# Cross-attention with Winograd products on one core: the last batch's closing order, and one reciprocal's place in the second batch

## The chip, the core and the metric

The kernel runs on one core of a Trainium2 chip. A core has five engines with instruction queues of their own: TensorE (PE; its weight loads are listed as PEld), VectorE (DVE), ScalarE (ACT), GpSimd (POOL) and SyncE (SP). Each works through its queue in order and waits on semaphores for the others. TensorE writes to eight PSUM banks, each of 128 partitions by 512 fp32 values; VectorE and ScalarE read and write the banks, and DMAs move data between the on-chip memory and HBM. The metric is the time on the device, in microseconds (us); the kernel before takes 672.67 us (median of three runs, 672.03 to 672.9).

## The reference

Eight batches of cross-attention, all in fp32. x1 is `x` and x2 is `ctx_2048`, both of shape (8, 512, 1024).

```python
q = jnp.einsum('bcn,dc->bnd', x1, Wq) + bq            # d = 64
k = jnp.einsum('bcn,dc->bdn', x2, Wk) + bk[:, None]
v = jnp.einsum('bcn,dc->bdn', x2, Wv) + bv[:, None]
attn = jax.nn.softmax(jnp.einsum('bnd,bdm->bnm', q, k), axis=2)
out = jnp.einsum('bcm,bnm->bcn', v, attn) + x1
```

For each of the 1024 columns n of x1, the scores against the 1024 columns m of x2 go through a softmax over m; the result is the weighted sum of the values, plus x1.

## The kernel before, in words

Batches are worked one after the other (`period(s, n, nn, nnn)`: s is the batch at hand, n, nn and nnn are the next ones), and every period also holds the scores, exponentials and first sums of batch n. The order of the instructions on each engine is written out by hand: instructions stand in each queue in the order in which the code calls them. Tiles are named by a tag, and a tile that takes a tag again waits until the tile before it has been read.

Two matrix products carry the work. First Y = x2 times the exponentials of the scores (`multiply`, `multiply_seeded` with stage "y"), then out = Wv times Y, scaled by the softmax's sums (stage "o"). Both are computed in 2 x 2 blocks by seven products in place of eight (Strassen's scheme in Winograd's form), in the order 1, 2, 6, 7, 5, 3, 4; some products are split in the same way once more (`inner_product`). Blocks are accumulated in PSUM: the pairs of banks "a0", "a1" and "c0", "c1" (the tags of `ps_a`), and two buffers "sc" (`ps_s`). Each bank of a pair holds one row tile j = 0, 1 of 128 rows by 512 columns. In the last batch `o_bank` swaps a and c in the second stage.

The last batch's second stage, as far as the change reaches: product 1 is put into bank pair c, product 6 is added to it and copied out by ScalarE (`s.tmp[6]`, tile `uo`), product 5 is added and copied out (`s.tmp[5]`, tile `uo`, L600), product 3 completes block 12 there. Product 7 is computed in pair a by `multiply_57` from inner products, interleaved with 5 and 3; VectorE completes its second row (L623). Block 22 is pair a plus `tmp[5]`; then product 4 is added to pair a, and block 21 is pair a plus `tmp[6]`. `evict_o` adds the bias and x1 (tile `s.x`, called `x_in_x_dram` in the trace), writes into that tile, and stores it with DMAs of 256 KB from SyncE. For blocks 22 and 21 it evicts both rows with bias and x1 (L739), then adds the parts and stores each row (L743, L744). TensorE's order there is product 3's first row, product 4 (both rows, L469), then product 3's second row in two halves (`rest`, L591), and block 12 is evicted last (L731), its second row in two halves, one stored by ScalarE and one by SyncE (L734).

In the second batch (`s.b == 1`) the sums of the softmax's denominators are reduced over partitions on GpSimd (L297), a small DMA takes 512 of them into a tile `few` of 128 x 4 (L299), VectorE inverts it (`invert`, L305, RECIPROCAL), GpSimd stores it as a row (L307), and `spread` reads it back to all partitions (L312). `shares` is both calls. Behind `shares(s, 1)` stand on VectorE the sums for the inner products of product 3: `right_stream` (L532, L537, L539, block sums of 128x1024 and 128x512) and `left_stream` (L517), which `weave` interleaves; then `lower` (L327), the completion of product 7 (`complete_7`, L661) and, on ScalarE, the negated copies of product 7 (`copy_7`, L671) and the copies between the inner steps of product 3 (L646).

Of the kernel before, what the change touches and what calls it, by code (L numbers as in the profile page):

```python
# [15 lines left out]
def kernel(  # L16
# [47 lines left out]
    nc = tc.nc  # L64
# [387 lines left out]
    def multiply(s, stage, i, left, right, n_k, last=False, hook=None, rows=range(2)):  # L452

        ka, kb, bank, opens = MULT[i]
        if stage == "o":
            bank = o_bank(s, bank)
            if i == 2:
                bank, opens = "p", False  # L460
        for j in rows:
            if opens:
                s.bank[bank, j] = ps_a.tile(
                    [P, H], F32, tag=f"{bank}{j}", name=f"ps_{stage}{bank}{j}_{s.b}_{i}"
                )
            ps = s.bank[bank, j]
            for n in HALVES if last and j else (slice(0, H),):
                for k in range(n_k):
                    nc.tensor.matmul(  # L469
                        ps[:, n],  # L470
                        left[ka][:, k, ts(j, P)],
                        right[kb][:, k, n],
                        start=opens and k == 0,
                        stop=i in (2, 3, 4) and k == n_k - 1,
                        skip_group_check=True,
                    )
# [100 lines left out]
    def multiply_57(s):  # L577

        s.inner["o7"] = inner_w["o7"]
        on, fresh = o_bank(s, "a"), o_bank(s, "c")  # L580
        bank = [ps_a.tile([P, H], F32, tag=f"{fresh}{j}", name=f"ps_o{fresh}{j}_{s.b}_7") for j in range(2)]
        s.bank[fresh, 0], s.bank[fresh, 1] = b0, b1 = bank
        chain, third = inner_parts(s, "o7")
        v = sb.tile([P, 2, H], F32, tag="aI3", name=f"vo7_{s.b}")[:, 0, left]
        s.tmp[5] = sb.tile([P, 2, H], F32, tag="u5", name=f"uo5_{s.b}")

        def plain(i, j, *ks, parts=(slice(0, H),)):
            ps, (ka, kb) = s.bank[on, j], (("S1", "T1"), ("S4", "22"))[i == 3]
            for n in parts:
                for k in ks:  # L590
                    nc.tensor.matmul(  # L591
                        ps[:, n],
                        w[ka][:, k, ts(j, P)],
                        s.y[kb][:, k, n],
                        start=False,
                        stop=i == 3 and k == 1,
                        skip_group_check=True,
                    )
            if i == 5 and 1 in ks:
                nc.scalar.copy(s.tmp[5][:, j, :], ps)  # L600
# [10 lines left out]
        nc.scalar.copy(b1[:, right], chain)  # L611
        plain(3, 0, 0)
        inner_product(s, "o7", 3, b0[:, right], False)
        plain(3, 0, 1)
        if s.b < B - 1:
            plain(3, 1, 0, 1)

        def rest():
            plain(3, 1, 0, 1, parts=HALVES)

        def complete():
            b = b1.rearrange("p (a n) -> p a n", a=2)
            nc.vector.tensor_tensor(b, b, v.unsqueeze(1).to_broadcast([P, 2, H // 2]), ALU.add)  # L623

        return complete, rest

    def multiply_seeded(s, i, v_tag, hooks={}, bank=None):

# [75 lines left out]
    def add_x1(s, k):  # L704

        nc.gpsimd.dma_start(s.tmp[RESULT[k][1]], block(s, k, x1), accum_op=ALU.add)

    def evict_o(s, k, hook=None):


# [4 lines left out]
        def bias(j):  # L715
            return bv_sb[:, 2 * r + j : 2 * r + j + 1]

        if s.b == B - 1 and k == "11":
            o = s.x[:, 0:2, ts(h, H)]
            for j in range(2):  # L720
                nc.vector.scalar_tensor_tensor(
                    o[:, j, :], s.bank[bank, j], bias(j), o[:, j, :], ALU.add, ALU.add
                )
                nc.sync.dma_start(out[s.b, ts(j, P), ts(h, H)], o[:, j, :])
            return
        if s.b == B - 1 and add is None:
            for j, n, engine in (
                (0, slice(0, H), nc.sync), (1, left, nc.scalar), (1, right, nc.sync)
            ):
                o = s.x[:, 2 * r + j, ts(h, H)][:, n]  # L730
                nc.vector.scalar_tensor_tensor(  # L731
                    o, s.bank[bank, j][:, n], bias(j), o, ALU.add, ALU.add
                )
                engine.dma_start(out[s.b, ts(2 * r + j, P), ts(h, H)][:, n], o)  # L734
            return
        if s.b == B - 1:
            o = s.x[:, 2 * r : 2 * r + 2, ts(h, H)]
            for j in range(2):
                nc.vector.scalar_tensor_tensor(  # L739
                    o[:, j, :], s.bank[bank, j], bias(j), o[:, j, :], ALU.add, ALU.add  # L740
                )
            for j in range(2):
                nc.vector.tensor_tensor(o[:, j, :], o[:, j, :], s.tmp[add][:, j, :], ALU.add)  # L743
# [20 lines left out]
        if hook is None and k in ("12", "22"):  # L764
            return leave
        leave()

    def add_tile(s, h, i):
        nc.gpsimd.dma_start(s.mx[h], s.e[h][:, :, i, :], accum_op=ALU.add)  # L769
# [148 lines left out]
    def period(s, n, nn, nnn):  # L918
# [7 lines left out]
        def second(i):  # L926
            if i == 1:
                multiply_o1(s)
            else:
                multiply(s, "o", i, w, s.y, 2, n is None and i == 3)  # L930

        def next_queries():
            evict = queries(nn, "c0")
# [98 lines left out]
        else:  # L1032
# [63 lines left out]
                s, 5, "r" if s.six else "top", {6: evict_q} if five else {}, "a"  # L1096
            )
            complete_5()
            shares(s, 1)
            if n is None:  # L1100
                for leave in s.leave:
                    leave()
            if n:
                weave(right_stream(s, 3, s.t["22"], "eT1"), left_stream(s, 3, s.a["S4"], "aI3"))
                lower(n, 0, 0)
            else:
                inner_right(s, 3, s.t["22"], "eT1")
# [140 lines left out]
                lower(n, 1, 3)  # L1248
                sum_y(s, "T4")
        if late:  # L1250
            complete_7, rest = multiply_57(s)
            if five:
                exponential(n, 1, 2)
                exponential(n, 1, 3)
# [84 lines left out]
```

## Time and profile before

| | |
|---|---|
| median of three runs | 672.67 us (672.03 to 672.9) |
| the profiled execution | 672.91 us |
| its span | 671.1 us |
| TensorE busy | 662.9 us, 99% |
| VectorE busy | 606.6 us, 90% |
| ScalarE busy | 363.2 us, 54% |
| GpSimd busy | 225.1 us, 34% |

The profiled execution's time is 1.8 us over its span. The span is the time from the first to the last event that the profiler recorded, and all positions below count from its start. A row of the timeline has the start, the time, the engine, the line of the kernel, the operation with what it writes and reads, its shape, how many instructions were merged, and in brackets the engine's idle time before it and what ended it. An fp32 matmul call shows as two matmul rows (two of 0.43 us for 512 columns). Rows with SPq or ACTq are DMA issues.

### The profile page before, as it was taken

To read this page: it belongs to the slowest core of one execution; us is meant where nothing else is said; L and a number is where in the kernel's file an instruction comes from. 1 tells how busy PE (TensorE), PEld (TensorE's weight loads), DVE (VectorE), ACT (ScalarE), POOL (GpSimd) and SP (SyncE) were. 2 spreads that over 40 slices of the span, in tenths; PEclk is the share of its full clock that TensorE was granted. 3 is DMA by queue.
4 is the path that set the end of the run, shared out by engine and by line. 5 is a ranking of instruction groups with operands and counts; after the bars stand their busy time and mean duration, and the time that the engine had idled before them with its cause. 6 is when DMAs were issued, how large, how long until landed. Compare 5 with 4: busy or idle time off the path is not lost.

```text
span 671.1 us, 7760 instructions
## 1 busy us (share of the span) xinstructions
PE 662.9 (99%) x2582; PEld 423.6 (63%) x2582; DVE 606.6 (90%) x828; ACT 363.2 (54%) x636; POOL 225.1 (34%) x196
## 2 busy tenths in 40 slices
PE   9999999999999999999999999999999999999996
PEld 5435754756558665677657685576855767566853
DVE  1989999899999899989999989998998988989974
ACT  2755466446565575464755647645576346554320
POOL 0125215630355312553134421454133450245300
PEclk9999999999999999999999999999999999999999
DMA  9679577995999859998699895999969990688522
GB/s 310 269 209 310 137 244 130 200 240 179 243 211 210 232 162 302 186 242 212 157 280 205 212 255 156 248 217 203 269 116 231 172 308 23 125 156 189 100 89 95
DMA packets 51960, 134.81 MB, mean 201 GB/s; under 512 B 5712, under 2 KB 8272, under 8 KB 51920
## 3 DMA queue, kind: packets, MB, share of 16 engines
q0 software_dynamic: 24480, 61.94, 50.8%
q1 hardware_dynamic: 27008, 71.97, 29.8%
q8 instruction: 21, 0.34, 0.2%
q10 hardware_dynamic: 432, 0.39, 0.2%
q14 instruction: 19, 0.16, 0.1%
HBM read 86.77 MB, written 16.81 MB: 154 GB/s over the span
## 4 chain that ended last, share of the span: by engine, by line
PE 77%; DVE 10%; POOL 4%; issue 3%; DMA 3%; ACT 1%; DVEq 0%; POOLq 0%; ACTq 0%
PE ps_yc L550 10%; PE ps_ya L550 7%; PE ps_oa L591 6%; PE ps_s L239 5%; PE ps_oa L469 4%; PE ps_o L469 4%; PE ps_oc L469 4%; PE ps_o L489 4%; PE ps_i4chain L550 3%; PE ps_k L191 3%; PE ps_i3chain L550 3%; PE ps_i5chain L550 2%; PE ps_i7chain L550 2%; PE ps_i2chain L550 2%; PE ps_i1chain L550 2%
## 5 line engine op out<-in xcount | busy, mean ns | idle before, releaser
L297 POOL PARTITION_ALL_REDUCE den<-sum x16 | 52.6, 3285 | 76.2 <-DVE sum L272 76.2
L327 DVE TENSOR_TENSOR e<-e,top 128x1024 f32<-128x1024 f32 x60 | 71.5, 1218 | 4.0 <-POOL top L278 4.0
L769 POOL DMA_DIRECT2D sum<-e x21 | 26.9, 1279 | 132.2 <-ACT sum L774 39.4
L336 ACT ACTIVATE e<-e 128x1024 f32<-128x1024 f32 x60 | 62.7, 1056 | 12.7 <-DVE e L327 12.0
L251 ACT COPY e<-ps_s 128x1024 f32<-128x1024 f32 x46 | 45.8, 1031 | 10.0 <-PE ps_s L239 6.5
L278 POOL PARTITION_ALL_REDUCE top<-max x16 | 31.8, 1991 | 56.3 <-DVE max L272 38.4
L239 PE MATMUL ps_s<-q,k 64*128 64x512 f32 (+1 forms) x192 | 48.0, 600 | 0.0
L262 DVE TENSOR_TENSOR max<-max,e 128x1024 f32<-128x1024 f32 x30 | 36.6, 1220 | 0.2
L239 PEld LDWEIGHTS ps_s<-q,k 64*128 64x128 f32 x192 | 17.1, 186 | 21.0 <-issue 15.6
L646 ACT COPY ps_ya<-ps_i1chain 128x256 f32<-128x256 f32 x28 | 10.0, 358 | 37.0 <-PE ps_i1chain L550 33.5
L683 DVE TENSOR_TENSOR y<-y,den 128x1024 f32<-128x1024 f32 x24 | 29.5, 1247 | 0.2
L489 PE MATMUL ps_o<-y,w 128*128 128x512 f32 x64 | 28.8, 592 | 0.0
L469 PE MATMUL ps_oc<-yT,w 128*128 128x512 f32 x64 | 28.8, 592 | 0.0
L469 PE MATMUL ps_oa<-yT,w_S 128*128 128x512 f32 x64 | 28.8, 592 | 0.0
L469 PE MATMUL ps_o<-y,w 128*128 128x512 f32 x64 | 28.8, 592 | 0.0
L312 POOL DMA_DIRECT2D den<-row x16 | 8.9, 558 | 58.1 <-DMA row<-few 39.7
L761 POOL DMA_DIRECT2D r<-in_x_dram x14 | 26.9, 1920 | 3.3 <-ACT r L749 2.3
L517 DVE TENSOR_TENSOR aI<-a 128x256 f32<-128x256 f32 x60 | 27.9, 485 | 0.0
L646 ACT COPY ps_yc<-ps_i7chain 128x256 f32<-128x256 f32 x32 | 11.4, 357 | 30.2 <-PE ps_i7chain L550 26.1
L517 DVE TENSOR_TENSOR aI<-a,aI 128x256 f32<-128x256 f32 x60 | 25.4, 423 | 1.3
L191 PE MATMUL ps_q<-x_in_x_dram,wqk_sb 128*64 128x512 f32 x112 | 25.6, 598 | 0.0
L646 ACT COPY ps_ya<-ps_i5chain 128x256 f32<-128x256 f32 x32 | 11.4, 357 | 26.1 <-PE ps_i5chain L550 22.0
(283 smaller groups left out, 1777.8 us busy)
## 6 DMA issues: line engine op xcount, KB each, us to landing
x_in_x_dram<-in_x_dram SPq DMA_DIRECT2D x60, 512.0 KB, 8.0
a<-in_x2T_dram SPq DMA_DIRECT2D x32, 512.0 KB, 10.1
sum<-e POOLq DMA_DIRECT2D x21, 512.0 KB, 6.4
aS<-in_x2T_dram POOLq DMA_DIRECT2D x19, 512.0 KB, 8.8
eT<-eT POOLq DMA_DIRECT2D x16, 512.0 KB, 10.6
uo<-in_x_dram POOLq DMA_DIRECT2D x14, 512.0 KB, 9.7
r<-in_x_dram POOLq DMA_DIRECT2D x14, 512.0 KB, 10.0
e<-e POOLq DMA_DIRECT2D x14, 512.0 KB, 10.3
```

Source lines behind the costliest of these rows:

```text
L191: nc.tensor.matmul(ps[r, :], w_sb[:, c, :], s.x[:, c, ts(h, H)], start=(c == 0), stop=(c == CT - 1),)
L239: nc.tensor.matmul(ps[g][:, n], s.k[r, ts(i, P)], s.q[r, ts(h, H)][:, n], start=True, stop=True)
L251: nc.scalar.copy(e[:, :, i, :], whole)
L262: nc.vector.tensor_tensor(f, e[:, :, 0, :] if i == 1 else f, e[:, :, i, :], op)
L297: nc.gpsimd.partition_all_reduce(s.den[h], s.mx[h][:, 0, :], P, ReduceOp.add)
L327: nc.vector.tensor_tensor(e, e, top, ALU.subtract)
L336: nc.scalar.activation(e, e, AF.Exp)
L469: nc.tensor.matmul(ps[:, n], left[ka][:, k, ts(j, P)], right[kb][:, k, n], start=opens and k == 0, stop=i in (2, 3, 4) and k == n_k - 1, s ...
L489: nc.tensor.matmul(ps, w["11"][:, k, ts(j, P)], s.y["11"][:, k, :], start=k == 0, stop=False, skip_group_check=True)
L517: nc.vector.tensor_tensor(v[k], v[x], v[y], op)
L550: nc.tensor.matmul(ps, s.inner[i][ka][:, k, :], s.inner[i, "t"][kb][:, k, :], start=opens and k == 0, stop=z in (2, 3, 4) and k == n_k - 1 ...
L591: nc.tensor.matmul(ps[:, n], w[ka][:, k, ts(j, P)], s.y[kb][:, k, n], start=False, stop=i == 3 and k == 1, skip_group_check=True,)
```

## The change

In the last batch four adds of `tmp[6]` (block 21) and `tmp[5]` (block 22) onto x1 are put ahead of product 7's completion on VectorE (`with_x1`). Blocks 22 and 12 are then evicted in one step for each row, and stored by SyncE. Product 3's second row is multiplied whole, right behind its first row. Product 4 comes last (`finish`): its first row is accumulated onto bank a0 as before, its second row goes in two halves to two fresh banks (tag c0 and a buffer "sc"). VectorE first adds the bias and bank a1 to x1's second row, then evicts the first row, then adds the two halves from the fresh banks; each piece is stored by SyncE as it is done, the halves with 128 KB each.

In the second batch `shares(s, 1)` is called behind the first block sum of `right_stream` (L532) instead of ahead of it. In the later batches the order of the sums stays as it was: the right sum, then left and right in turn.

```diff
@@ multiply_57
         plain(3, 0, 0)
         inner_product(s, "o7", 3, b0[:, right], False)
         plain(3, 0, 1)
-        if s.b < B - 1:
-            plain(3, 1, 0, 1)
-
-        def rest():
-            plain(3, 1, 0, 1, parts=HALVES)
+        plain(3, 1, 0, 1)
...
+    def with_x1(s, k, j):
+        r, h = int(k[0]) - 1, int(k[1]) - 1
+        x = s.x[:, 2 * r + j, ts(h, H)]
+        nc.vector.tensor_tensor(x, x, s.tmp[RESULT[k][1]][:, j, :], ALU.add)
...
@@ evict_o, last batch
-            o = s.x[:, 2 * r : 2 * r + 2, ts(h, H)]
             for j in range(2):
-                nc.vector.scalar_tensor_tensor(
-                    o[:, j, :], s.bank[bank, j], bias(j), o[:, j, :], ALU.add, ALU.add
-                )
-            for j in range(2):
-                nc.vector.tensor_tensor(o[:, j, :], o[:, j, :], s.tmp[add][:, j, :], ALU.add)
-                nc.sync.dma_start(out[s.b, ts(2 * r + j, P), ts(h, H)], o[:, j, :])
+                o = s.x[:, 2 * r + j, ts(h, H)]
+                nc.vector.scalar_tensor_tensor(o, s.bank[bank, j], bias(j), o, ALU.add, ALU.add)
+                nc.sync.dma_start(out[s.b, ts(2 * r + j, P), ts(h, H)], o)
             return
...
+    def finish(s):
+        bank = o_bank(s, "c")
+        tiles = (
+            (0, slice(0, H), s.bank[bank, 0], False),
+            (1, left, ps_a.tile([P, H], F32, tag=f"{o_bank(s, 'a')}0", name="ps_last1"), True),
+            (1, right, ps_s.tile([P, 2, H], F32, tag="sc", name="ps_last2")[:, 0, :], True),
+        )
+        for j, n, ps, opens in tiles:
+            for k in range(2):
+                nc.tensor.matmul(
+                    ps[:, n], w["22"][:, k, ts(j, P)], s.y["T4"][:, k, n],
...
+                )
+        o = [s.x[:, 2 + j, 0:H] for j in range(2)]
+        nc.vector.scalar_tensor_tensor(o[1], s.bank[bank, 1], bv_sb[:, 3:4], o[1], ALU.add, ALU.add)
+        nc.vector.scalar_tensor_tensor(o[0], s.bank[bank, 0], bv_sb[:, 2:3], o[0], ALU.add, ALU.add)
+        nc.sync.dma_start(out[s.b, ts(2, P), 0:H], o[0])
+        for n, ps in ((left, tiles[1][2]), (right, tiles[2][2])):
+            nc.vector.tensor_tensor(o[1][:, n], o[1][:, n], ps[:, n], ALU.add)
+            nc.sync.dma_start(out[s.b, ts(3, P), n], o[1][:, n])
...
@@ period, second and later batches
             complete_5()
-            shares(s, 1)
+            if s.b > 1:
+                shares(s, 1)
...
             if n:
-                weave(right_stream(s, 3, s.t["22"], "eT1"), left_stream(s, 3, s.a["S4"], "aI3"))
+                sums_3 = right_stream(s, 3, s.t["22"], "eT1")
+                next(sums_3)
+                if s.b == 1:
+                    shares(s, 1)
+                weave(left_stream(s, 3, s.a["S4"], "aI3"), sums_3)
                 lower(n, 0, 0)
...
@@ period, the end of the last batch
+        if n is None:
+            for k in ("21", "22"):
+                for j in range(2):
+                    with_x1(s, k, j)
         if late:
             complete_7()
...
         else:
-            second(4)
-            evict_o(s, "21")
-            rest()
             evict_o(s, "12")
+            finish(s)
```

More of the change, by code (lines that the diff above doesn't have):

```diff
@@ L450, in o_bank, with multiply @@
         return {"a": "c", "c": "a"}.get(bank, bank) if s.b == B - 1 else bank
-    def multiply(s, stage, i, left, right, n_k, last=False, hook=None, rows=range(2)):
+    def multiply(s, stage, i, left, right, n_k, hook=None, rows=range(2)):
         ka, kb, bank, opens = MULT[i]
@@ L466, in multiply @@
             ps = s.bank[bank, j]
[L467 to L475, printed above, removed]
-                    )
+            for k in range(n_k):
+                nc.tensor.matmul(
+                    ps,
+                    left[ka][:, k, ts(j, P)],
+                    right[kb][:, k, :],
+                    start=opens and k == 0,
+                    stop=i in (2, 3, 4) and k == n_k - 1,
+                    skip_group_check=True,
+                )
             if i in (1, 6, 5):
@@ L716, in bias @@
             return bv_sb[:, 2 * r + j : 2 * r + j + 1]
[L718 to L719 removed]
+        if s.b == B - 1:
             for j in range(2):
[L721 to L744 removed]
+                o = s.x[:, 2 * r + j, ts(h, H)]
+                nc.vector.scalar_tensor_tensor(o, s.bank[bank, j], bias(j), o, ALU.add, ALU.add)
+                nc.sync.dma_start(out[s.b, ts(2 * r + j, P), ts(h, H)], o)
             return
```

35 lines of the change are left out of this document (21 added, 14 removed).

## The prediction

> **What bounds the kernel now.** I read the page first, then the chain of work that ended last, then the timeline around the two places that the change touches, then the waits and the DMA view there.
>
> ```profile
> span 671.1 us, 7760 instructions
> ...
> PE 662.9 (99%) x2582; PEld 423.6 (63%) x2582; DVE 606.6 (90%) x828; ACT 363.2 (54%) x636; POOL 225.1 (34%) x196
> ```
>
> TensorE is busy for 99% of the span, so only two things can shorten the kernel: a gap in TensorE's stream that closes, or the stretch after its last matmul. The change touches one of each. The timeline of the last batch's end:
>
> ```profile
> 656.32 0.59 ACT L600 COPY uo<-ps_oc 128x512 f32<-128x512 f32 x1 [0.93 <-PE ps_oc L591]
> ...
> 657.57 0.70 DVE L623 TENSOR_TENSOR ps_oa<-ps_oa,vo 128x512 f32<-128x512 f32 x1 [5.66 <-ACT ps_oa L611]
> ...
> 658.27 1.02 PE L591 MATMUL ps_oc<-y,w_S 128*128 128x512 f32 x2
> 658.47 1.41 DVE L739 SCALAR_TENSOR_TENSOR x_in_x_dram<-ps_oa,bv_sb,x_in_x_dram 128x512 f32<-128x512 f32 x2 [0.20 <-PE ps_oa L550]
> 659.27 0.30 PEld L469 LDWEIGHTS ps_oa<-yT,w 128*128 128x128 f32 x2 [0.81 <-DVE x_in_x_dram L739]
> 659.27 3.70 PE L469 MATMUL ps_oa<-yT,w 128*128 128x512 f32 x8
> 659.79 1.28 DVE L743 TENSOR_TENSOR x_in_x_dram<-x_in_x_dram,uo 128x512 f32<-128x512 f32 x2
> ...
> 662.81 1.89 PE L591 MATMUL ps_oc<-y,w_S 128*128 128x256 f32 x8
> ...
> 664.88 1.53 DVE L731 SCALAR_TENSOR_TENSOR x_in_x_dram<-ps_oc,bv_sb,x_in_x_dram 128x512 f32<-128x512 f32 x3
> 665.66 1.12 SPq L734 DMA_DIRECT2D out_dram<-x_in_x_dram  x2
> ```
>
> Matmuls end at 664.70 (662.81 + 1.89), VectorE at 666.41 (664.88 + 1.53), and SyncE's last issue at 666.78. So VectorE closes 1.71 us after the last matmul, because three of its instructions queue behind block 21's adds. The chain says the same: it leaves TensorE at 662.99, while matmuls still run, and goes on through VectorE alone.
>
> ```profile
> 659.29 3.70 PE ps_oa L469 x8
> ...
> 665.63 0.78 DVE x_in_x_dram L731 x2
> ```
>
> Behind VectorE come the stores. The first two rows are the tile's view with the issue times, then issues with their median time to landing (640 to 672 us), then the instruction queue's share in 666.0 to 666.5, then two windows of DMA rate (last column).
>
> ```profile
> L734 SPq DMA_DIRECT2D out_dram<-x_in_x_dram x2: 333/333/333, 665.7 to 666.4; - x2
> ...
> out_dram<-x_in_x_dram SPq DMA_DIRECT2D x7, 256.0 KB, 2.1
> out_dram<-x_in_x_dram ACTq DMA_DIRECT2D x1, 128.0 KB, 3.6
> out_dram<-x_in_x_dram SPq DMA_DIRECT2D x1, 128.0 KB, 3.5
> ...
> q8 instruction: 1, 0.02, 11.6%
> ...
> 667.00:668.00 1.00, 0.00 (x0) 0.00 (x0) 0.00 (x0) 0.00 (x0) 0.00 (x0) 1.00 1.01 341
> 668.00:669.00 1.00, 0.00 (x0) 0.00 (x0) 0.00 (x0) 0.00 (x0) 0.00 (x0) 1.00 0.13 46
> ```
>
> The last store (128 KB) is issued at 666.45 (666.78 less its 0.33) and lands 3.5 us later, at 669.95. The usual 256 KB store needs 2.1. The last ones wait behind each other (all engines busy in 667 to 668), and then one engine trails: 46 GB/s in 668 to 669. The instruction fetch fits that: 11.6% of 16 engines over 0.5 us is 0.93 us of one engine. From 669.95 to the span's end are 1.2 us.
>
> Now the second batch, around the moved reciprocal (timeline), and the same instructions a batch later:
>
> ```profile
> 141.89 3.26 DVE L532 TENSOR_TENSOR eI7yT<-e 128x1024 f32<-128x1024 f32 x1
> ...
> 149.16 0.68 DVE L661 TENSOR_TENSOR ps_ya<-ps_ya,v 128x512 f32<-128x512 f32 x1
> ...
> 149.34 1.77 POOL L278 PARTITION_ALL_REDUCE top<-max  x1 [3.38 <-DVE max L272]
> ...
> 152.45 0.18 DVE L305 RECIPROCAL few<-few 128x4 f32<-128x4 f32 x1 [2.60 <-DMA few<-den]
> 152.54 1.20 DVE L532 TENSOR_TENSOR eI3eT<-e 128x1024 f32<-128x1024 f32 x1
> ...
> 156.94 1.03 PE L550 MATMUL ps_i3chain<-eI3eT,aI 128*128 128x256 f32 x4
> 157.14 0.37 ACT L646 COPY v<-ps_i3third 128x256 f32<-128x256 f32 x1 [0.45 <-PE ps_i3third L550]
> 157.46 0.69 DVE L661 TENSOR_TENSOR ps_yc<-ps_yc,v 128x512 f32<-128x512 f32 x1
> ...
> 157.81 1.03 PE L550 MATMUL ps_yc<-e,aS 128*128 128x256 f32 x4
> ...
> 158.19 0.60 ACT L671 ACTIVATE uy<-ps_yc 128x512 f32<-128x512 f32 x1 [0.67 <-DVE ps_yc L661]
> 158.81 0.36 ACT L646 COPY ps_yc<-ps_i3chain 128x256 f32<-128x256 f32 x1
> ...
> 159.22 1.13 PE L550 MATMUL ps_i3chain<-eI3eT,aI 128*128 128x256 f32 x4 [0.39 <-ACT ps_yc L646]
> ```
>
> ```profile
> 231.53 1.78 POOL L278 PARTITION_ALL_REDUCE top<-max  x1 [5.28 <-DVE max L272]
> ...
> 232.03 1.61 DVE L532 TENSOR_TENSOR eI3eT<-e 128x1024 f32<-128x1024 f32 x1
> ```
>
> VectorE stands 2.60 us at the reciprocal, until a small DMA lands at 152.4. Everything behind is late, product 7's completion (L661, 157.46) with it; ScalarE waits 0.67 for that, and its next copy holds TensorE. Four-matmul groups start 0.87 apart (156.94, 157.81), so the next was due at 158.68; it starts at 159.22. That is 0.54 us lost by the engine that bounds the kernel.
>
> **The change, part by part.** *Second batch.* One 128x1024 subtraction is put ahead of the reciprocal; no instruction is added, and POOL's queue keeps its order. The subtraction starts where VectorE now goes idle, about 149.75 (149.16 + 0.68 less the usual overlap). Beside POOL's reduction, as in the batch after, it takes 1.61, to 151.4. The reciprocal is due at 152.45 as before, so the row that it stores, and the wait of POOL behind it, do not move. All behind it on VectorE comes one subtraction earlier: 152.54 instead of 153.66, 1.1 us. L661 then ends at 157.05 instead of 158.15, before ScalarE has finished the copy of 157.14 to 157.51. ScalarE's negated copy runs 157.51 to 158.11, the copy that TensorE needs to about 158.45, and TensorE goes on at 158.68. Gain 0.54. The costliest such subtraction beside a reduction is the row at 141.89 (3.26). It would end at 153.0 and leave half of the 1.1; L661 would end at 157.6, the copy at 158.6, still in time. So the bounds are 0 (the gain is eaten later) and 0.6 (the stalled group also took 0.1 longer).
>
> The Trainium skill ("SBUF — State Buffer", section "Who interferes with whom") speaks against this part: a VectorE instruction with two SBUF inputs and a GpSimd instruction that reads SBUF lock each other out for a whole instruction. By it the subtraction would start only when the reduction ends (149.34 + 1.77 = 151.11) and end at 152.3, still ahead of 152.45, so its sum is the same with the spare time down from 1.0 us to 0.1. The trace does not bear out a full lock: in the later batch the subtraction ended at 233.64, 0.33 after the reduction, and not 1.2 after it.
>
> *Last batch, VectorE.* Four adds of parts onto x1, 128x512 from SBUF, at 0.64 each (L743's pair is 1.28), go into the 5.66 us that VectorE idles ahead of 657.57 (from 651.9). The parts of product 6 are there long before; the second part of product 5 ends on ScalarE at 656.91. So three adds are done by 654.2, and the fourth runs from 656.95 to 657.6. Behind it waits product 7's completion, now at 657.57: cost 0.05, and that goes into the 0.20 us that block 22's first eviction waits for TensorE anyway. Block 22's two evictions end at 659.88 as now, and L743's adds after them are gone. If this cover were missing, 2.56 us would stand at the end.
>
> *Last batch, TensorE.* Eight calls before and after, with the same columns. Product 3's second row moves ahead of product 4, unsplit. The 0.27 that TensorE loses at 659.27 (3.70 for 3.43; it waits for block 22's eviction) goes, as product 4 now comes 1.72 later, when that bank is long read. Starts: product 3 row two at 659.13, product 4 row one at 660.85, the halves of row two at 662.57 and 663.43; end 664.45. The fresh bank of the left half is free once block 12's first row is read (659.88 + 0.75 = 660.63), 1.9 us early.
>
> *Last batch, the close.* VectorE: block 12's rows at 659.88 and 661.05 (product 3 done at 661.0); block 21's second row with bias, without product 4, 661.8 to 662.5; its first row 662.77 to 663.52; left half to 664.1; right half from 664.48. An add of 128x256 from a bank has no row. The half evictions of L731 take about 0.39 each (1.53 less 0.75, by two), a 128x512 add 0.64; I take 0.45, and 0.39 to 0.64 moves the end by under 0.2. VectorE ends at 664.93 instead of 666.41, and the last store issues at 664.96 instead of 666.45: gain 1.49.
>
> *Last batch, stores.* Nine stores before and after; ScalarE's one goes to SyncE, whose issue of 0.33 fits between VectorE's ends (at least 0.58 apart). The stores at 663.55 (256 KB), 664.1 and 664.96 (128 KB each) now come about as slowly as they drain, so the last should land like a lone one. The upper bound is its present 3.5, the lower about 1.7 (256 KB take 0.77 us at the 341 GB/s of 667 to 668, and half of that comes off 2.1). I take 2.1, the row of lone 256 KB stores: nearer to the lone case, with something left for the instruction fetch. It lands at 667.05 instead of 669.95: 2.9 in all for the close, between 1.5 and 3.3.
>
> The Trainium skill ("DMA: Bandwidth & Descriptors", section "Anatomy of one DMA — SWDGE (gpsimd) path") fits a DMA as about 2.0 us plus bytes at 436 GB/s, an estimate of 2.3 for this store; by that the sum would be 0.2 smaller. It would give 2.6 for 256 KB, where this trace has 2.1 on SyncE's queue.
>
> *Sum.* 0.54 + 2.9 = 3.4 us off the profiled execution's 672.91 (its span and 1.8 around it): 669.5. That execution lies 0.24 over the median of 672.67, so the median should come to about 669.3.
>
> **The rivals.** *The fetch hits the last store.* It came 1.55 us after the last matmul; so it would come at 666.0, while the last store's data move. Then that lands 0.93 later, the gain is 2.5, the time 670.2.
>
> *The closed gap is given back,* by a wait later that hangs on DMA and not on TensorE. Against it, TensorE has no idle time in the windows behind (window, length, then TensorE's busy time):
>
> ```profile
> 180.00:270.00 90.00, 90.00 (x347) 58.28 (x346) 85.09 (x119) 53.17 (x93) 32.09 (x30) 1.00 0.91 225
> ...
> 540.00:630.00 90.00, 89.95 (x342) 61.84 (x339) 82.96 (x119) 46.70 (x87) 31.74 (x31) 1.00 0.63 140
> ```
>
> The close alone remains: 669.8.
>
> *The stores land no sooner:* 3.5 us after issue, as the last two do now. Gain 1.5, and with the gap given back: 671.2, on the edge of no change. For it speaks that the stores' spacing is only estimated; against it, that five of them are out before the last three.
>
> *Slower:* everything after 159 us comes 0.54 sooner while some stores do not. VectorE then waits longer for the tile that block 12's store still reads:
>
> ```profile
> 221.64 1.23 DVE L532 TENSOR_TENSOR eI5u<-eT 128x1024 f32<-128x1024 f32 x1 [2.88 <-DMA out_dram<-uo]
> ...
> 225.41 0.81 PE L550 MATMUL ps_i5third<-eI5u,aI 128*128 128x256 f32 x3
> ```
>
> TensorE needs it at 225.41 and has it at 222.87: 2.54 to spare. From there each microsecond of a later store costs one. To lose the close's 2.9 and be 1.35 slower (674.0), the stores of the middle batches must together come some 4.3 us beyond that spare time. Nothing in the trace moves them so far.
>
> **How the numbers follow.** About 0.2% (1.35 us) is what a measurement of this kernel tells from no change. Forecast 0.58 (668.5 to 670.0), fetch 0.16, gap given back 0.10, stores no sooner 0.10, slower 0.06. The first three are faster: 0.84. Same 0.10, slower 0.06. The low end, 668.5, is the close at 3.3, the gap at 0.6 and the runs' own spread; the high end, 671.2, takes in the third rival.
>
> **What would show it.** Right: no VectorE wait over 1.2 us at the reciprocal, no TensorE wait behind ScalarE near 159; VectorE's last end within 0.6 us of the last matmul's, no wait of product 4 for block 22's eviction; last store landing about 2.1 after issue. Wrong: a fourth add that holds product 7's completion, a TensorE wait on a fresh bank, a last store that lands 3 us or more after issue, or a new TensorE wait in a middle batch.

## The result and the profile after

The changed kernel takes 670.48 us at the median (669.72 to 672.46), the kernel before, run beside it, 673.38 (671.69 to 675.29). The ratio is 0.9961 with a 95% interval of 0.9951 to 0.997: 2.9 us off by the medians, 2.6 by the ratio, between 2.0 and 3.3 by the interval. The forecast was 3.4 off, to 669.3. The time lies above the forecast's narrow band (668.5 to 670.0) and within its whole range (668.5 to 671.2); the kernel before was itself 0.7 slower beside this run than the 672.67 that the forecast started from. Two terms of the sum are wrong, in opposite directions; the experiments below take them apart.

The page of the changed kernel's profiled execution (670.53 us):

```profile
span 668.8 us, 7761 instructions
...
PE 663.3 (99%) x2582; PEld 423.8 (63%) x2582; DVE 608.6 (91%) x829; ACT 363.1 (54%) x636; POOL 224.9 (34%) x196
```

The timeline of the last batch's end, in the changed kernel:

```profile
657.07 0.58 ACT L598 COPY uo<-ps_oc 128x512 f32<-128x512 f32 x1 [0.93 <-PE ps_oc L589]
...
657.68 0.69 DVE L706 TENSOR_TENSOR x_in_x_dram<-x_in_x_dram,uo 128x512 f32<-128x512 f32 x1 [2.75 <-ACT uo L598]
...
658.32 0.70 DVE L617 TENSOR_TENSOR ps_oa<-ps_oa,vo 128x512 f32<-128x512 f32 x1
...
659.02 2.74 PE L589 MATMUL ps_oc<-y,w_S 128*128 128x512 f32 x6
659.22 1.41 DVE L721 SCALAR_TENSOR_TENSOR x_in_x_dram<-ps_oa,bv_sb,x_in_x_dram 128x512 f32<-128x512 f32 x2 [0.20 <-PE ps_oa L549]
...
661.60 1.88 PE L756 MATMUL ps_oa<-yT,w 128*128 128x512 f32 x4
...
663.31 1.89 PE L756 MATMUL ps_last<-yT,w 128*128 128x256 f32 x8
663.51 0.75 DVE L766 SCALAR_TENSOR_TENSOR x_in_x_dram<-ps_oa,bv_sb,x_in_x_dram 128x512 f32<-128x512 f32 x1 [0.31 <-PE ps_oa L756]
...
664.38 0.42 DVE L769 TENSOR_TENSOR x_in_x_dram<-x_in_x_dram,ps_last 128x256 f32<-128x256 f32 x1
664.83 1.20 SPq L770 DMA_DIRECT2D out_dram<-x_in_x_dram  x2
665.24 0.42 DVE L769 TENSOR_TENSOR x_in_x_dram<-x_in_x_dram,ps_last 128x256 f32<-128x256 f32 x1 [0.44 <-PE ps_last L756]
```

The fourth add (L706 at 657.68) waits for ScalarE's copy, and product 7's completion (L617) stands right behind it. Block 22's eviction (659.22) still waits 0.20 us for TensorE, so the add costs nothing. No matmul row has a wait in brackets: the 0.27 us at product 4 are gone, and the fresh banks (`ps_last`) are free in time. Matmuls end at 665.20 (663.31 + 1.89), VectorE at 665.66, and the chain of waits now stays on TensorE up to its last matmul:

```profile
663.48 1.74 PE ps_last L756 x8
665.22 0.02 issue
665.24 0.42 DVE x_in_x_dram L769
```

The stores of the close by the DMA view (655 to 669 us; KB each, median us from issue to landing), then the last store alone, and the only instruction fetch there, in the window 657.0 to 657.5:

```profile
out_dram<-x_in_x_dram SPq DMA_DIRECT2D x5, 256.0 KB, 2.1
out_dram<-x_in_x_dram SPq DMA_DIRECT2D x2, 128.0 KB, 2.0
...
out_dram<-x_in_x_dram SPq DMA_DIRECT2D x1, 128.0 KB, 1.9
...
q8 instruction: 1, 0.02, 12.6%
```

From the last matmul to the span's end are 3.6 us (668.8 less 665.20). Before, they were 6.4 (671.1 less 664.70).

The second batch, by the timeline of the changed kernel:

```profile
148.39 1.03 PE L549 MATMUL ps_ya<-eI5u,aS 128*128 128x256 f32 x4
...
150.57 1.77 POOL L278 PARTITION_ALL_REDUCE top<-max  x1 [3.38 <-DVE max L272]
...
150.99 1.69 DVE L531 TENSOR_TENSOR eI3eT<-e 128x1024 f32<-128x1024 f32 x1
...
154.30 0.18 DVE L305 RECIPROCAL few<-few 128x4 f32<-128x4 f32 x1 [1.62 <-DMA few<-den]
...
158.18 0.69 DVE L655 TENSOR_TENSOR ps_yc<-ps_yc,v 128x512 f32<-128x512 f32 x1
158.91 0.60 ACT L665 ACTIVATE uy<-ps_yc 128x512 f32<-128x512 f32 x1 [0.45 <-DVE ps_yc L655]
...
159.95 1.13 PE L549 MATMUL ps_i3chain<-eI3eT,aI 128*128 128x256 f32 x4 [0.17 <-ACT ps_yc L640]
...
166.37 3.65 PE L191 MATMUL ps_k<-x_in_x_dram,wqk_sb 128*64 128x512 f32 x16
```

The subtraction (L531) has moved ahead of the reciprocal and took 1.69 us beside the reduction. Yet VectorE still waits 1.62 us at the reciprocal, and TensorE still waits behind ScalarE at 159.95. To measure the loss free of the start's shift, take the stretch from the first row of that fence to the last. Undisturbed it is 17.54 us (the experiments show it several times). Here it is 17.98, a loss of 0.44 (the brackets show only 0.17 of it as idle time). Before, the same two rows were:

```profile
147.45 1.03 PE L550 MATMUL ps_ya<-eI5u,aS 128*128 128x256 f32 x4
...
165.65 3.65 PE L191 MATMUL ps_k<-x_in_x_dram,wqk_sb 128*64 128x512 f32 x16
```

That is 18.20, a loss of 0.66. So this execution gained 0.22 us here and not 0.54.

The two spans add up so: 0.22 in the second batch, 0.25 on TensorE in the last batch (22.33 us before, 22.08 after), 2.8 in the close, less 0.9 by which the changed kernel's execution was late from its start (its hundredth matmul starts at 19.2 instead of 18.3, and the group above at 148.39 instead of 147.45). That is 2.4, as the spans say. The hundredth matmul starts at 18.3, 19.3 and 20.5 us in three profiles of the kernel before, so the 0.9 is not of the change.

### The profile page after: what moved, and what is told of

Read it like the earlier page. It is cut to its first block, busy times and chain, and to the rows that moved or that the text cites. A ratio compares the mean times of both kernels' runs of the same rounds, so it can differ in the third digit from the quotient of the medians.

```text
span 668.8 us, 7761 instructions
## 1 busy us (share of the span) xinstructions
PE 663.3 (99%) x2582; PEld 423.8 (63%) x2582; DVE 608.6 (91%) x829; ACT 363.1 (54%) x636; POOL 224.9 (34%) x196
## 4 chain that ended last, share of the span: by engine, by line
PE 92%; DMA 3%; DVE 2%; issue 1%; POOL 1%; ACT 1%; ACTq 0%; DVEq 0%; POOLq 0%
PE ps_yc L549 11%; PE ps_ya L549 7%; PE ps_oa L589 6%; PE ps_s L239 6%; PE ps_oa L468 5%; PE ps_oc L468 5%; PE ps_o L468 4%; PE ps_o L488 4%; PE ps_k L191 3%; PE ps_q L191 3%; PE ps_i4chain L549 3%; PE ps_ya L468 3%; PE ps_i3chain L549 3%; PE ps_i5chain L549 3%; PE ps_i2chain L549 3%; PE ps_i1chain L549 3%
## 5 line engine op out<-in xcount | busy, mean ns | idle before, releaser
L516 DVE TENSOR_TENSOR aI<-a 128x256 f32<-128x256 f32 x60 | 25.8, 451 | 0.0
```

What stands on the lines that cost most here:

```text
L516: nc.vector.tensor_tensor(v[k], v[x], v[y], op)
```

## The experiments

Two questions: what each half of the change is worth, and why the reciprocal's half gave less in the profile. Theory at first: the close carries some 2.9 us, because VectorE ends earlier and the last store has the queues to itself; the reciprocal's move carries about half a microsecond. Rivals: the store term is the work of one fetch that fell into the last stores, and not of the close; the gap that closes at 159 us is given back later.

**The last batch alone.** The changed kernel with `shares(s, 1)` back ahead of the block sum:

```diff
-            if s.b > 1:
-                shares(s, 1)
+            shares(s, 1)
...
-                if s.b == 1:
-                    shares(s, 1)
```

> The last batch's part alone; the reciprocal of the second batch stands ahead of the block sum as before. Theory (the close carries the gain): 2.9 to 3.2 us faster than before, so within 0.5 us of the changed kernel; the wait of TensorE near 159 us is back (0.5 to 0.6 us lost there), VectorE ends within 0.6 us of the last matmul and the last store lands about 2 us after its issue. Rival (the second batch carries a good part): less than 2 us faster than before.

Measured: 671.61 us, ratio 0.9967 (0.9952 to 0.9982), some 2.2 us faster than before by that ratio, where 2.9 to 3.2 were expected. In its profile the small DMA landed early, and TensorE had no wait near 159 us although the old order was back: that expectation missed too, and it showed that the wait there depends on the execution. TensorE waited elsewhere, in the last period, at 605 us (below).

**The reciprocal alone.** The kernel before, with the order of the second batch changed as in the change:

```diff
-            shares(s, 1)
+            if s.b > 1:
+                shares(s, 1)
...
-                weave(right_stream(s, 3, s.t["22"], "eT1"), left_stream(s, 3, s.a["S4"], "aI3"))
+                sums_3 = right_stream(s, 3, s.t["22"], "eT1")
+                next(sums_3)
+                if s.b == 1:
+                    shares(s, 1)
+                weave(left_stream(s, 3, s.a["S4"], "aI3"), sums_3)
```

> The second batch's part alone. Theory: 0.2 to 0.55 us faster than before, by as much as the small DMA that the reciprocal waits for lets it; the last batch's end is as before (VectorE ends 1.7 us after the last matmul, the last stores land 3 to 4 us after issue). Rival (the gap is given back later): TensorE's lead after 160 us is gone by 600 us and the time is that of before.

Measured: 672.66 us, ratio 0.9989 (0.9977 to 1.0): 0.7 us faster, at the edge of what can be told from nothing. No TensorE wait at 159 us; in its profile TensorE loses 0.8 us at 605 us instead (below). The last stores land 2.2 to 2.3 us after issue, where 3 to 4 were expected. With the run above, the halves add to 2.9 us by the ratios, beside 2.6 for the whole change: no sign, within these intervals, that they interact.

**The reciprocal behind all sums of product 3.**

```diff
                 next(sums_3)
+                weave(left_stream(s, 3, s.a["S4"], "aI3"), sums_3)
                 if s.b == 1:
                     shares(s, 1)
-                weave(left_stream(s, 3, s.a["S4"], "aI3"), sums_3)
```

> The changed kernel with the reciprocal of the second batch moved behind all seven block sums of product 3. Theory (the small DMA lands later or sooner by about 1 us from run to run, and one sum does not always cover it): VectorE no longer waits at the reciprocal, TensorE has no wait behind ScalarE near 159 us, and TensorE gains about 0.55 us there against before, 0.3 us more than in the profile of the changed kernel; the row and its spread come 2 us later and are still in time. Rival (the spread of the second half's reciprocals then comes late): VectorE waits at the scaling by den around 171 us and TensorE loses 1 us or more behind it.

Measured: 670.7 us, ratio 0.9955 (0.9939 to 0.9972). VectorE no longer waits at the reciprocal, and TensorE loses nothing at 159 us, nor from there to 600 us, so the rival on the late spread does not hold. By its time it is not told apart from the changed kernel.

**The adds alone.** The kernel before with the four adds moved ahead, its order of products and its evictions otherwise kept:

```diff
-            for j in range(2):
-                nc.vector.tensor_tensor(o[:, j, :], o[:, j, :], s.tmp[add][:, j, :], ALU.add)
                 nc.sync.dma_start(out[s.b, ts(2 * r + j, P), ts(h, H)], o[:, j, :])
...
+        if n is None:
+            for k in ("21", "22"):
+                for j in range(2):
+                    with_x1(s, k, j)
```

> The kernel before with only the four adds onto x1 put ahead of product 7's completion; products, evictions and the two halves stay in the old order, the second half stored by ScalarE as before; the second batch as before. Theory (the close was held by VectorE's adds): VectorE ends about 0.9 us after the last matmul in place of 1.7 us, the stores of block 21 leave 0.7 to 1.3 us sooner, and the kernel is 1.5 to 2.3 us faster than before, so about two thirds of the close's gain. Rival (the order of the products carries it): under 0.7 us faster than before.

Measured: 672.98 us, ratio 0.9989 (0.9977 to 1.0002): 0.7 us faster, where 1.5 to 2.3 were expected. The timeline of its end:

```profile
664.88 1.89 PE L591 MATMUL ps_oc<-y,w_S 128*128 128x256 f32 x8
...
665.75 0.74 DVE L737 SCALAR_TENSOR_TENSOR x_in_x_dram<-ps_oc,bv_sb,x_in_x_dram 128x512 f32<-128x512 f32 x1
...
666.81 0.88 DVE L737 SCALAR_TENSOR_TENSOR x_in_x_dram<-ps_oc,bv_sb,x_in_x_dram 128x256 f32<-128x256 f32 x2 [0.32 <-PE ps_oc L591]
```

Matmuls end at 666.77, and both half evictions start only then, though the left half's matmuls end 0.86 us sooner: the eviction of a half waits for the bank's last matmul. Whether the chip or the program's own semaphores make it wait, no run tells. VectorE ends 0.92 after, the stores land 1.9 us after issue, and the span (670.8) ends 4.0 after the last matmul. So the mechanism is there. What was wrong was the measure: against the 6.4 us of the one profile of before, 4.0 looks like 2.4 gained; the next run shows that 6.4 was not usual.

**The kernel before again,** unchanged, for a second profile.

> The kernel before, profiled once more, to see which of its waits are its own and which are that one execution's. Theory (the last stores queue behind each other): they land 3.5 us after issue again. Rival (the 16 KB instruction fetch at 666.25 us, in the middle of the last stores, made most of that): with the fetch elsewhere they land 2.0 to 2.5 us after issue, and the span behind the last matmul is about 5.1 us in place of 6.4. The wait near 159 us is expected between 0 and 1.5 us, by when the small DMA lands.

Measured: 672.5 us, span 670.7. Its last matmuls and its last two stores:

```profile
663.59 1.89 PE L591 MATMUL ps_oc<-y,w_S 128*128 128x256 f32 x8
```

```profile
out_dram<-x_in_x_dram ACTq DMA_DIRECT2D x1, 128.0 KB, 2.3
out_dram<-x_in_x_dram SPq DMA_DIRECT2D x1, 128.0 KB, 2.2
```

The stores land 2.2 to 2.3 us after issue and not 3.5, no instruction fetch falls into them, and from the last matmul (665.48) to the end are 5.2 us. The run with the reciprocal alone, which has the old close too, shows 5.2 as well. So the rival on the fetch holds: of the 6.4 us, 1.2 stood in one execution only.

**No fresh banks.** The changed kernel, with product 4's second row accumulated in halves onto bank a1:

```diff
-            (1, left, ps_a.tile([P, H], F32, tag=f"{o_bank(s, 'a')}0", name="ps_last1"), True),
-            (1, right, ps_s.tile([P, 2, H], F32, tag="sc", name="ps_last2")[:, 0, :], True),
...
+        for j, n in ((0, slice(0, H)), (1, left), (1, right)):
+            ps = s.bank[bank, j]
...
-        nc.vector.scalar_tensor_tensor(o[1], s.bank[bank, 1], bv_sb[:, 3:4], o[1], ALU.add, ALU.add)
...
-            nc.vector.tensor_tensor(o[1][:, n], o[1][:, n], ps[:, n], ALU.add)
+            nc.vector.scalar_tensor_tensor(
+                o[1][:, n], s.bank[bank, 1][:, n], bv_sb[:, 3:4], o[1][:, n], ALU.add, ALU.add
+            )
```

> The changed kernel without the fresh banks: product 4's second row is accumulated in two halves onto bank a1, and each half is evicted with bias and x1 in one step. Theory (the fresh banks let VectorE take the left half while TensorE fills the right one): both evictions now wait for the last matmul, VectorE ends 0.85 to 0.95 us after it in place of 0.46, and the kernel is 0.3 to 0.5 us slower than the changed one (2.2 to 2.8 us faster than before). Rival (the fresh banks bring nothing): the same close as the changed kernel.

Measured: 671.28 us, ratio 0.9967 (0.9952 to 0.9981). The timeline of its end:

```profile
661.05 3.61 PE L752 MATMUL ps_oa<-yT,w 128*128 128x512 f32 x12
...
664.70 0.87 DVE L764 SCALAR_TENSOR_TENSOR x_in_x_dram<-ps_oa,bv_sb,x_in_x_dram 128x256 f32<-128x256 f32 x2 [0.98 <-PE ps_oa L752]
```

Both halves wait for the last matmul (664.66) and VectorE ends 0.91 after it, where the changed kernel's ends 0.46 after. The stretch to the end is 4.1 instead of 3.6. The fresh banks are worth about that half microsecond. With the adds alone, above, the stretch was 4.0, so the new order of the products by itself shortens nothing behind the last matmul.

**The second row whole,** in one fresh bank, evicted and stored in one piece:

```diff
-            (1, left, ps_a.tile([P, H], F32, tag=f"{o_bank(s, 'a')}0", name="ps_last1"), True),
-            (1, right, ps_s.tile([P, 2, H], F32, tag="sc", name="ps_last2")[:, 0, :], True),
+            (1, slice(0, H), ps_a.tile([P, H], F32, tag=f"{o_bank(s, 'a')}0", name="ps_last1"), True),
...
-        for n, ps in ((left, tiles[1][2]), (right, tiles[2][2])):
+        for n, ps in ((slice(0, H), tiles[1][2]),):
```

> The changed kernel with product 4's second row whole in one fresh bank, one add of 128x512 and one store of 256 KB behind it. Theory: VectorE ends 0.7 us after the last matmul in place of 0.46, the last store lands 2.1 us after issue in place of 1.9: 0.3 to 0.6 us slower than the changed kernel. Rival (a whole row saves a wait and a DMA): the same or faster.

Measured: 670.85 us, ratio 0.9972 (0.9961 to 0.9984). The timeline:

```profile
664.10 1.88 PE L755 MATMUL ps_last<-yT,w 128*128 128x512 f32 x4
...
666.01 0.69 DVE L768 TENSOR_TENSOR x_in_x_dram<-x_in_x_dram,ps_last 128x512 f32<-128x512 f32 x1 [0.96 <-PE ps_last L755]
```

VectorE ends 0.72 after the last matmul, the 256 KB store lands 2.0 after issue, and the stretch is 4.0 us. Splitting the row is worth 0.4 to 0.5 by the profiles, less than the spread of the times.

**The kernel before and the adds alone, once more,** to see whether a fetch had made the adds look small:

> The kernel before with only the four adds moved, profiled once more, because its time (0.7 us faster than before) fell short of its close in the profile (3.7 us from the last matmul to the end, against 5.1 to 6.4 before). Theory (the instruction fetch sometimes meets its last stores): a stretch of 3.6 to 3.8 us where the fetch comes before the last stores, and 4.3 us or more where it meets them. Rival: the stretch is 3.7 us again and the fetch is not the cause.

> The kernel before, a third profile: from the last matmul to the end 5.1 to 5.4 us where the instruction fetch misses the last stores, about 6.4 us where it meets them; VectorE ends 1.71 us after the last matmul in any case.

Measured for the adds: 673.2 us, span 671.4, and again stores that land in 1.9 and 4.0 us from the last matmul to the end (the 3.7 in the expectation was a misreading: the first profile shows 4.0 too). The fetch came 7.5 and 7.7 us before the end, among the earlier stores. In the first of these profiles it came in the window 663.0 to 663.5, and a store issued at 662.0 landed 4.5 us later, at 666.5:

```profile
out_dram<-x_in_x_dram SPq DMA_DIRECT2D x1, 256.0 KB, 4.5
...
q8 instruction: 1, 0.02, 21.5%
```

The other profiles agree. In four of the fourteen the fetch met stores under way, and the slowest of these landed 3.7 us after issue (the first of before), 3.3 (the reciprocal alone), 4.5 and 4.0 (the adds alone). Every store that it did not meet, in any profile, landed within 2.4 us of its issue from 650 us on. So it is the fetch that made the last stores of the first profile late. With the adds alone it met earlier ones, which landed well before the last three, so it had not made the adds' gain small. TensorE lost 1.92 us in the second batch, 1.48 in the profile of the first such run. From stretches of 5.2 and 4.0 the adds are worth 1.2, which lies in the measured interval (−0.1 to 1.5); whether late small DMAs also told against these runs is open.

Measured for before: 676.53 us, span 674.8, 3 us later than the first profile of before by 60 us from the start, 5.2 us from the last matmul to the end, and the longest of the waits at the reciprocal:

```profile
150.50 1.03 PE L550 MATMUL ps_ya<-eI5u,aS 128*128 128x256 f32 x4
...
156.71 0.18 DVE L305 RECIPROCAL few<-few 128x4 f32<-128x4 f32 x1 [3.45 <-DMA few<-den]
...
163.48 1.13 PE L550 MATMUL ps_i3chain<-eI3eT,aI 128*128 128x256 f32 x4 [1.16 <-ACT ps_yc L646]
...
169.90 2.37 PE L191 MATMUL ps_k<-x_in_x_dram,wqk_sb 128*64 128x512 f32 x10
```

**What the second batch's loss hangs on.** The same rows can be read in every profile: lateness is the reciprocal's start less the start of the group `ps_ya<-eI5u,aS`, loss is the stretch from that group to `ps_k` less 17.54. For this last one 156.71 − 150.50 = 6.21, and 169.90 − 150.50 − 17.54 = 1.86. With the reciprocal where the change puts it, the run without fresh banks shows the early end:

```profile
148.34 1.03 PE L549 MATMUL ps_ya<-eI5u,aS 128*128 128x256 f32 x4
...
152.42 0.18 DVE L305 RECIPROCAL few<-few 128x4 f32<-128x4 f32 x1 [0.70 <-DMA few<-den]
...
165.88 3.65 PE L191 MATMUL ps_k<-x_in_x_dram,wqk_sb 128*64 128x512 f32 x16
```

Lateness 4.08, loss 0. All profiles:

| order | lateness and loss (us) |
|---|---|
| reciprocal first | 4.27 and 0; 4.83 and 0.49; 5.00 and 0.66; 5.82 and 1.48; 6.21 and 1.86; 6.26 and 1.92 |
| one sum ahead (the change) | 3.83 and 0; 4.08 and 0; 5.91 and 0.44; 5.95 and 0.48; 6.04 and 0.56 |
| all sums ahead | 6.05, 6.45 and 6.94, each 0 |

In the first two rows the reciprocal starts when the small DMA has landed, so lateness is the DMA's. In the third it waits for nothing: there lateness is its later place in VectorE's queue. The loss is what the lateness has over 4.34 in the old order, and over 5.48 in the new one. The threshold moved by 1.14 us; the prediction's "one subtraction earlier" was 1.1. The lateness varies by itself, in both orders over the same range, because the small DMA is issued 1.7 to 3.0 us ahead of that group and lands 6.8 to 7.9 us after its issue. Averaged over the eleven latenesses of the first two rows, the old order would lose 1.03 and the new one 0.30: an estimate of 0.73 us for the reciprocal's half, beside 0.7 measured for it alone (0 to 1.5 by its interval).

**The wait at 605 us.** Some profiles showed a TensorE wait in the last period. VectorE's fold there (L272) waits for a GpSimd DMA that sums a tile of exponentials (`sum<-e`) and stands behind three others. In the run of the last batch alone, which had no loss at 159:

```profile
600.72 1.03 PE L549 MATMUL ps_ya<-e,a 128*128 128x256 f32 x4
...
604.78 0.69 DVE L272 TENSOR_TENSOR sum<-sum 128x512 f32<-128x512 f32 x1 [2.19 <-DMA sum<-e]
...
606.63 1.13 PE L549 MATMUL ps_i2chain<-eI2eT,aI 128*128 128x256 f32 x4 [0.57 <-ACT ps_yc L640]
...
611.26 7.11 PE L468 MATMUL ps_ya<-eT,aS 128*128 128x512 f32 x16
```

The stretch from the first of these rows to the last is 10.54 us; undisturbed it is 9.50, so this execution lost 1.04. And in its DMA view (580 to 606 us):

```profile
sum<-e POOLq DMA_DIRECT2D x1, 512.0 KB, 13.2
```

Is this the closed gap, given back? To test it, the DMA was issued earlier, ahead of the others, with the reciprocal behind all sums:

```diff
             weave(folds(n, 1, "max", ALU.max), right_stream(s, "o7", s.y["T3"], "eT1"))
+            add_tile(n, 0, 3)
             highest(n, 1)
...
         if n:
-            if not nn:
-                add_tile(n, 0, 3)
```

> The kernel with the reciprocal behind all sums of product 3, and in the seventh batch's period GpSimd issues the accumulation of the fourth exponential tile onto the sum ahead of the maximum's reduction, so ahead of three other DMAs, instead of behind them. Theory (the gain of the second batch is given back near 605 us, where VectorE waits for that accumulation and TensorE behind it): VectorE no longer waits at the fold of the sum there, TensorE has no wait near 605 us, and the kernel is 0.5 to 0.9 us faster than with the later reciprocal alone, 3.3 to 4.2 us faster than before. Rival (the wait at 605 us was that run's accident, or another DMA takes its place): the same time as with the later reciprocal alone.

Measured: 670.11 us, ratio 0.9961 (0.9947 to 0.9976), span 667.6: some 2.6 us faster than before by the ratio, where 3.3 to 4.2 were expected. The timeline and the DMA view:

```profile
601.28 0.68 DVE L272 TENSOR_TENSOR sum<-sum 128x512 f32<-128x512 f32 x1
```

```profile
sum<-e POOLq DMA_DIRECT2D x1, 512.0 KB, 5.0
```

The DMA lands in 5.0 us, the fold waits for nothing, and TensorE waits neither at 159 nor at 605. But the wait at 605 is not the gap given back. The run without fresh banks has a loss at neither place; the third profile of before has it at both, late at 159 by 1.86 and still with this wait in its timeline:

```profile
607.72 0.69 DVE L272 TENSOR_TENSOR sum<-sum 128x512 f32<-128x512 f32 x1 [1.79 <-DMA sum<-e]
```

Of the twelve profiles without that last edit, four (the last batch alone, the reciprocal alone, the reciprocal behind all sums, the third of before) lose 0.6 to 1.0 us at 605, and the others at most 0.1. Three of these four lost nothing at 159, so a link between the two is not ruled out by counting. The DMA's times speak against one: in every one of the twelve it is issued at the same point of TensorE's stream, 9.2 us ahead of the row `ps_ya<-e,a`, so a gain at 159 moves it along. Its landing varies, and the fold starts 2.6 to 4.1 us after that row (4.06 in the fence above). The loss is what this has over 3.02, or nothing. So it is the same kind of wait as at 159: a landing that varies, against a threshold. The first of the three DMAs ahead of it (`a<-in_x2T_dram`) took 6.6 to 7.4 us in the four profiles and 5.1 to 5.7 in the others; why is open.

**The changed kernel and the last version, side by side.**

> The changed kernel once more, beside the one with the later reciprocal and the earlier accumulation. Theory: 2 to 3.3 us faster than before; the last store lands 1.8 to 2.1 us after issue, the stretch from the last matmul to the end is 3.5 us as in every kernel with the new close; the loss of TensorE near 159 us is (time of the reciprocal after the group of product 5's first matmuls, less 5.48 us), or nothing.

> The kernel with the later reciprocal and the earlier accumulation once more. Theory: no TensorE wait near 159 us and none near 605 us whatever the small DMA does; 0.2 to 0.7 us faster than the changed kernel, which loses 0.1 to 0.2 us at 159 us on average and up to 0.9 us at 605 us in some executions. Rival: those waits are too rare to show, and the two have the same time.

Measured: the changed kernel 670.87 us, ratio 0.9951 (0.9935 to 0.9967); with the earlier DMA and the reciprocal behind all sums 670.36, ratio 0.9947 (0.9934 to 0.9959). The first lost 0.56 at 159 with a lateness of 6.04, as the formula in its expectation gives; the second waited at neither place. The medians point the same way (670.36 here and 670.11 above, against 670.87 here and 670.48 at first), but the intervals overlap: that the waits are gone is shown, that the time is shorter is not.

## Why the prediction was right, and where it was not

*What bounds the kernel* was read rightly. TensorE is at 99% in both profiles; the gains came from a stall of it and from the stretch behind its last matmul.

*The adds.* Right. They fit into VectorE's idle time; the fourth delays product 7's completion and costs nothing, because of the 0.20 us that block 22's eviction waits anyway.

*TensorE in the last batch.* Right: 0.25 against the predicted 0.27, no wait for a fresh bank.

*VectorE's close.* Right: its end is 0.46 us after the last matmul against 0.48, and the 128x256 add from a bank took 0.42 against the 0.45 taken from rows nearby.

*The stores.* The new value was nearly right (the last store landed in 1.9 us against 2.1), the old one mis-sized: this is the first failed step. The 3.5 us of the last store was read from one execution, in which the instruction fetch fell into the last stores. The prediction saw that fetch and priced it at 0.93, but took it as part of the kernel before. In the other three profiles with the old close the last store landed in 2.2 us and not 3.5, and from the last matmul to the end were 5.2 us and not 6.4. So the stores' term, predicted at 1.4, measures 0.4 (from 2.24 to 1.85 us, issue to landing). The close is worth 5.2 less 3.6, or 1.6, and TensorE's 0.25 with it 1.9 us; the prediction had 2.9. The adds carry 1.2 of it, the fresh banks about 0.5, and the new order gives TensorE's 0.25. By the Trainium skill ("DMA: Bandwidth & Descriptors", section "Anatomy of one DMA — SWDGE (gpsimd) path") the estimate for the last store was 2.3 us; the 1.9 measured on SyncE's queue lies under it.

*The second batch.* The mechanism was right and its shift was sized rightly (1.1 against 1.14). The failed step is "the reciprocal is due at 152.45 as before": the DMA that sets it lands at another time in each execution, by up to 2.4 us against TensorE (lateness 3.83 to 6.26). In the profile of the changed kernel it came 0.9 later than before and left a loss of 0.44 where none was predicted; on average the old order loses more than the 0.54 of the profile read, and the move is worth about 0.7 and not 0.54. That lies over the prediction's upper bound of 0.6, which rested on one lateness. Two of its signs of being right failed here: VectorE waited 1.62 us at the reciprocal, where 1.2 was the most, and TensorE waited behind ScalarE near 159.

*The sum.* 1.6 + 0.25 + 0.73 makes 2.6 us, an estimate from these profiles, against 2.9 by the medians, 2.6 by the ratio (2.0 to 3.3), and 3.4 predicted. The 0.3 between the sum and the medians is within the interval; late stores in the old close (1.2 us, in one of four profiles) may be part of it, which is not shown. The second batch's term was 0.2 too small and so offset a fifth of the 1.0 by which the close was too large; that is luck.

*The rivals.* The fetch did not hit the last store of the new close. The stores did land sooner. The gap was not given back at 605 us: the wait there comes and goes with a DMA that is issued along with TensorE's stream. And no store of a middle batch held the kernel up: from the row `ps_k` to the row `ps_ya<-e,a` TensorE took 434.18 us before (165.65 to 599.83) and after (166.37 to 600.55).

*The lock.* By the Trainium skill ("SBUF — State Buffer", section "Who interferes with whom") the subtraction would have started at the reduction's end. The trace does not agree: it started at 150.99 and ended at 152.68, only 0.34 after the reduction (150.57 + 1.77), and the reduction kept its length. It did take 1.69 where 1.20 is its time alone.

## What to carry to other kernels

One profile gives one draw of everything that hangs on DMA: before a late landing goes into a sum, look for it in a second execution, or in the same operation elsewhere in the trace, and ask whether a fetch or other traffic stood beside it. A wait whose releaser varies is worth its average loss over the threshold, and an edit that moves the threshold is worth the difference of two averages, not the stall of one trace. At the end of a kernel, move what needs no last matmul ahead of it, and give the last pieces banks of their own, since here an eviction of half a bank waited for the whole bank's matmuls.

## What the hardware showed that was not expected

- An instruction fetch of 16 KB held the share of one DMA engine for about a microsecond (12.6% of 16 engines over 0.5 us is 1.0 us here, 0.93 in the profile of before), and the last stores beside it landed 3.5 us after issue against 2.2 to 2.3 without it. It fell into the last stores in one of four profiles with the old close and in none with the new one, where it comes about 8 us before the last matmul's end. In three other profiles it met earlier stores, and the slowest of these landed after 3.3 to 4.5 us while the rest were not late. What sets its time is open.
- The DMA of 2 KB ahead of the moved reciprocal took 6.8 to 7.9 us from issue to landing. The same DMA of other batches (`few<-den`) took 1.9 us at 126 us and 2.0 at 607 us in the profile of before, so the size does not set it.
- A DMA of 512 KB (`sum<-e`) landed 11.8 to 13.2 us after issue behind three others on its queue, and 5.0 us after issue ahead of them, some 8 us earlier in TensorE's stream.
